# A selective-scan kernel: the product with B made in place, for two tiles in one GpSimd instruction

## The chip, the cores and the metric

The kernel runs on one core of a Trainium2 chip. Its engines each work through their own list of instructions in order and wait for one another by semaphores: TensorE (PE in the profile; its weight loads are PEld), VectorE (DVE), ScalarE (ACT), GpSimd (POOL) and SyncE (SP), whose queue here issues nearly all DMA transfers. The metric is the device time of one execution in microseconds. Three runs of the kernel before took 11,110.65, 11,111.8 and 11,118.07 us; the median is 11,111.8 us.

## What is computed

The input `x` is a batch of 8 images of 64 x 64 pixels with 96 channels, all float32. The reference applies two residual layers.

```python
# layer 0: x = x + SS2D(group_norm(x))
xz = einsum('bhwc,ec->bhwe', x, in_proj_w); xc, z = split(xz)      # 192 channels each
xa = silu(depthwise_conv3x3(xc) + conv_b)
xs = four orders of the 4096 pixels: rows, columns, and both reversed    # K = 4
x_dbl = einsum('bkdl,kcd->bkcl', xs, x_proj_w)                     # 6 dt rows, 16 B rows, 16 C rows
delta = softplus(dt_proj(dts) + dt_proj_b)
A = -exp(A_logs)                                                   # (K, 192, 16)
# at each of 4096 steps, for 192 channels x 16 states:
h = exp(delta * A) * h + (delta * u) * B
y = sum over the 16 states of h * C;   out = y + u * D
# the four orders are added, layer-normed, gated by silu(z), projected back to 96 channels

# layer 1: x = x + MLP(group_norm(x)), with up- and down-sampling by FFT filters around
h = coef0 + coef1 * (W1 x + b1) + coef2 * (W1 x + b1)**2;   W2 h + b2
```

Nearly all of the time goes to the scan `h = exp(delta * A) * h + (delta * u) * B`, which has 8 images x 4 orders x 192 channels x 16 states x 4096 steps.

## The kernel before

**Tiles.** One tile of the scan is 128 partitions by T = 1024 steps: 8 channels times 16 states. 192 channels make NT = 24 tiles for a chunk of 1024 steps; 4 chunks, 4 orders and 8 images make 3072 tiles in a row, in the list `tiles`. Each tile has a number `i` within its chunk, and the tiles of a chunk share a dictionary `got` with the chunk's inputs: `du` (delta times u, 192 x 1024, in DRAM), `dl` (delta), `br` and `cr` (the 16 rows of B and of C, repeated for the 8 channels, 128 x 1024 each).

**The steps of a tile.**
- `fetch` (line 1059): SP issues a DMA that reads 8 rows of `du` from DRAM and writes each of them 16 times, into the SBUF tile `dub`, 128 x 1024 (512 KB).
- `product_b` (1067): POOL multiplies `dub` by `br` into `bb`.
- `decay` (1071): PE spreads delta over the states by four matmuls into a PSUM tile `pd`, and ACT takes the exponential with the scale `neg_a`, in place.
- `scan` (1084): DVE runs the recurrence with `pd` as the factor and `bb` as the term. The result stays in `pd`, or goes to the SBUF tile `h` where the tile is marked `by_pool`: every third one (`i % 3 == 2`).
- `product_c` (1093): the result times `cr` gives `hc`. POOL does this for `by_pool` tiles, DVE for the others, 2048 of 3072.
- `hold` (1104): the last column is copied to `carry`, by ACT for `by_pool` tiles and else by DVE.
- `sums` (1119): PE adds the 16 states of two tiles at a time into the PSUM tile `py`; after eight tiles `store` copies it out.

**The order of the work** is written out by hand: the whole program is under a manual schedule, and the loop over `i` in its last part emits the steps of several tiles in each pass. In pass i, in this order: the loads of `before` where `i % 8 == 4`; the fetch of tile i + 6 (`FETCH`); `product_c` of tile i - 1 if it is POOL's; `product_b` of tile i + 3 (`LEAD`); `decay` of tile i + 1; `scan`, DVE's `product_c` and `hold` of tile i; then side work; and, in odd passes, `sums` of tiles i - 3 and i - 2. Two tiles of `pd` exist, four of `dub`, four of `bb`, four of `hc`, two of `h`.

**Side work.** The class `Side` holds generators for everything else: the loads, norms and convolutions of the next image (`front`), the layer norm and projection of the image before (`tail`), its MLP (`mlp`), and the preparation of the next chunk (`prepare`: `u`, `br`, `cr`, delta and `du`). A pass emits as many of their steps as a budget of estimated engine times (`CAPS`) allows. Where a pass gives PE too little, `turn_over` adds a matmul that nobody uses. The transfers of this side work are in SP's queue between the fetches.

**Buffers and waits.** Semaphore waits are derived from the use of tiles: a tile from a ring of four can be written again when the readers of the one four places before are done. So `fetch` of tile t waits for `product_b` of tile t - 4, and `product_b` of tile t waits for the scan of tile t - 4. A transfer also waits for the landing of the one that used its semaphore before; eight semaphores go round.

The functions that the change touches:

Of the kernel before, what the change touches and what calls it, by code (L numbers as in the profile page):

```python
# [8 lines left out]
F32 = mybir.dt.float32  # L9
AF = mybir.ActivationFunctionType  # L10
ALU = mybir.AluOpType
# [8 lines left out]
NS = 16  # L20
R = 6
K = 4
T = 1024
# [113 lines left out]
def kernel(ctx: ExitStack, tc: tile.TileContext, a: dict, out: bass.AP):  # L137
    nc = tc.nc
# [92 lines left out]
    sp = ctx.enter_context(tc.tile_pool(name="scan", bufs=3))  # L231
# [39 lines left out]
    def constants_in():  # L271
        nc.gpsimd.memset(xp, 0.0)
        raw["sel"] = tile_([128, 8, 128], "sel_0")
        for hf in range(2):
            nc.sync.dma_start(
                raw["sel"][64 * hf : 64 * hf + 64].rearrange("p j m -> p (j m)"),
                a["sel_b"][0:64, 0:2].rearrange("r q j m -> r (q j m)"),
            )
        raw["dt_b"] = tile_([C, K, HF], "dt_b")
        nc.sync.dma_start(raw["dt_b"], a["dt_b"])  # L280
        names = ("xp_dt", "xp_c", "xp_b")
        raw["xp"] = [tile_([128, K, Q3, R if n == "xp_dt" else NS], n) for n in names]
        ds = raw["ds"] = tile_([128, Q3, K], "ds")
        for hf in range(2):
            for q, r0, r1, f, c0 in pieces:
                rows, src = slice(64 * hf + r0, 64 * hf + r1), slice(c0, c0 + r1 - r0)
                for t, name in zip(raw["xp"], names):
                    nc.sync.dma_start(t[rows, :, q, :], a[name][src, :, f, 0 : t.shape[-1]])
                nc.sync.dma_start(ds[rows, q, :], a["ds"][src, f, :])
        for name, shape in (("coef", [128, 3, 3]), ("w2", [128, 3, C]), ("b2", [128, C])):  # L290
            raw[name] = tile_(shape, name)
            nc.sync.dma_start(raw[name], a[name])
# [748 lines left out]
    tiles = []  # L1041
    for b in range(images):
        for k in (1, 0, 2, 3):
            order = range(NCH) if k < 2 else range(NCH - 1, -1, -1)
            for n, c in enumerate(order):
                got = {}
                for i in range(NT):
                    q, n8 = divmod(i, 8)
                    s, j = n8 % 2, n8 // 2
# [6 lines left out]

    summed = set()

    def fetch(t):
        assert t["got"]["ready"]  # L1060
        t["dub"] = sp.tile([128, T], F32, tag="dub", name="dub", bufs=4)
        g = t["g"]
        nc.sync.dma_start(
            t["dub"], t["got"]["du"][None, 8 * g : 8 * g + 8, :].to_broadcast([NS, 8, T])
        )

    def product_b(t):
        t["bb"] = sp.tile([128, T], F32, tag="bb", name="bb", bufs=4)
        nc.gpsimd.tensor_tensor(t["bb"], t["dub"], t["got"]["br"], ALU.mult)  # L1069

    def decay(t):
        pd = t["pd"] = psd.tile([128, T], F32, tag="pd", name="pd")
        for hf in range(2):
            rows = slice(64 * hf, 64 * hf + 64)
            nc.tensor.matmul(  # L1075
                pd[:, MB * hf : MB * hf + MB],
                sel_b[rows, 4 * t["s"] + t["j"]].rearrange("p n c -> p (n c)"),
                t["got"]["dl"][rows, t["q"], :],
                start=True,
                stop=True,  # L1080
            )
        nc.scalar.activation(pd, pd, AF.Exp, scale=neg_a[:, t["k"], t["g"] : t["g"] + 1])  # L1082
# [10 lines left out]
    def product_c(t):  # L1093
        t["hc"] = sp.tile([128, T], F32, tag="hc", name="hc", bufs=4)
        (nc.gpsimd if t["by_pool"] else nc.vector).tensor_tensor(t["hc"], t["h"], t["got"]["cr"], ALU.mult)  # L1095
# [45 lines left out]
    def before(t):  # L1141

        if t["k"] == 0:
            return
        yp = t["got"]["yp"] = sp.tile([128, MB], F32, tag="yp", name="yp", bufs=2)
        if t["k"] == 1:
            q = t["q"]
            src = [
                u_dram[t["b"]][1][64 * q : 64 * q + 64, t["i0"] + MB * hf : t["i0"] + MB * hf + MB]
                for hf in range(2)  # L1150
            ]
        else:
            src = parts(t)
        for hf in range(2):
            nc.sync.dma_start(yp[64 * hf : 64 * hf + 64], src[hf])
# [14 lines left out]
    LEAD, FETCH = 3, 6  # L1170

    with tc.manual_schedule():
        side.queue = [bp.open("setup")]
        side.drain()
        constants_in()
        start, rest = front(0)
        side.queue = start[:-4]
        side.drain()
        side.queue = start[-4:] + [(8, 0, constants_of_scans), (8, 0, constants_of_mlp)]
        side.drain()  # L1180
        side.urgent = prepare(0, tiles[0]["k"], tiles[0]["i0"], tiles[0]["got"])
        side.queue, rest = rest[:4], rest[4:]
        while side.urgent or side.hurried:
            side.advance({e: (2 * most, 2 * most) for e, (_, most) in Side.CAPS.items()}, 2, 0)
        n = len(tiles)
        for i in range(FETCH):
            fetch(tiles[i])
            if i >= FETCH - LEAD:
                product_b(tiles[i - FETCH + LEAD])
        decay(tiles[0])  # L1190
        begin, *side.later = prepare(0, tiles[NT]["k"], tiles[NT]["i0"], tiles[NT]["got"])
        total = 1
        for i in range(n + 4):
            t = tiles[i] if i < n else None
            at = i % (NT * NCH * K)
            if t and t["i"] == 0:
                b = t["b"]
                if at == 0:
                    y_dram[b] = [dr.tile([DI, L], F32, tag=f"y{o}", name=f"y{o}") for o in range(2)]
                    side.begun, hasty = 0, sum(item[1] for item in rest) if b == 0 else 0  # L1200
                    side.queue += rest
                    down, end = [], []
                    if b:
                        keep = {}
                        side.queue += tail(b - 1, keep)
                        up, down, end = mlp(b - 1, keep)
                        side.queue += up
                    if b + 1 < images:
                        start, rest = front(b + 1)
                        side.queue += start[:2] + [i for two in zip(down, start[2:10]) for i in two] if b else start[:10]  # L1210
                        side.queue += start[10:] + rest
                        rest = []
                    else:
                        side.queue += down
                    side.queue += end
                    total = sum(item[1] for item in side.queue)
                if b == images - 1 and at == NT * NCH * (K - 1):
                    keep = {}
                    side.queue += tail(b, keep, pairs=False)
                    total = 0  # L1220

            ahead = 4 if i < 2 * NT else 8
            if (i + ahead) % NT == 0 and i + ahead + NT < n:
                nxt = tiles[i + ahead + NT]
                begin, *side.later = prepare(nxt["b"], nxt["k"], nxt["i0"], nxt["got"])
                side.urgent.append(begin)

            if i == 2:
                side.urgent.append(begin)
            if i == 4 or i and i % NT == 0:  # L1230
                side.urgent += side.later
                side.later = []
            if t and t["i"] % 8 == 4:
                before(t)
            if i + FETCH < n:
                fetch(tiles[i + FETCH])
            if 0 < i <= n and tiles[i - 1]["by_pool"]:
                product_c(tiles[i - 1])
            if i + LEAD < n:
                product_b(tiles[i + LEAD])  # L1240
            if i + 1 < n:
                decay(tiles[i + 1])
            if t:
                scan(t)
                if not t["by_pool"]:
                    product_c(t)
                hold(t)
            ends = i % 2 == 1 and 3 <= i <= n + 2
            adds = ends and tiles[i - 2]["j"] == 3 and tiles[i - 2]["k"]
            side.advance(  # L1250
                Side.CAPS,
                2 if not total or side.begun < max(hasty, total * at / 290) else 0,
                0 if 7 <= i % NT <= 21 else 1,
                0.95 * (bool(ends) + bool(adds)),
            )
            turn_over()
            if ends:
                sums(tiles[i - 3 : i - 1])
                if tiles[i - 2]["j"] == 3:
                    side.stores.append([g := store(tiles[i - 2]), next(g)])  # L1260
        up, down, end = mlp(images - 1, keep)
        side.queue += up + down + end
        side.drain()
# [89 lines left out]
```

## Time and profile before

| what | value |
|---|---|
| median of three runs | 11,111.8 us |
| profiled execution, from its first instruction to its last | 11,105.8 us |
| DVE busy | 10,207.5 us (92%) |
| POOL busy | 10,179.6 us (92%) |
| PE busy | 9967.9 us (90%) |
| ACT busy | 5910.6 us (53%) |
| DMA queue of SP | 86.5% of 16 engines' span, 2391.45 MB |
| `bb` products on POOL | 3072 of 2359 ns, 7173.5 us |
| `hc` products on POOL | 1024 of 2357 ns, 2413.9 us |
| scans on DVE | 3072 of 2280 to 2350 ns in four groups, 7163.7 us |
| `hc` products on DVE | 2048 of 1225 ns, 2508.4 us |

The profile is of one execution. It gives the time from its first to its last instruction; this is the profiled execution's own time in what follows, and the runs' median is 6 us above it. Busy time of an engine is the union of its instructions; waiting and issuing are not in it. In a line of a group of instructions, the part before the bar names line, engine, operation, output and inputs with their shapes and count; after it stand the busy time, the mean duration in ns, and the idle time of the engine just before these instructions with what ended it. In a line of waits, "DVE pd L1089 <- ACT carry L1108: 203.2, 414, 3.6" says that DVE's instruction at line 1089 sat idle until ACT's at line 1108 was done, for 203.2 us in total, 414 times, 3.6 us at most. "SPq" and the like are the engine's queue, in which it waits and issues.

### The profile page before, as it was taken

What the parts mean: (1) busy time and instruction counts of PE and PEld (TensorE: products, weight loads), DVE (VectorE), ACT (ScalarE), POOL (GpSimd) and SP (SyncE); (2) the same over time, 40 slices, a digit from 0 to 9 for tenths busy, and PEclk for the clock granted to TensorE, in tenths of its full rate; (3) what the DMA queues carried; (4) which work ended last, traced back from release to release, by engine and by line L of the source; (5) the groups of instructions that cost most, each with busy time, mean ns of one, the idle gap of its engine ahead of it and who ended that gap; (6) DMA issues with size and microseconds to landing.
All of it is one profiled execution on the core that took longest, in us unless ns stands there. A gap on an engine that the chain in (4) does not pass through costs nothing. (4 is left out here: it accounts for less than half of the span.)

```text
span 11105.8 us, 137238 instructions
## 1 busy us (share of the span) xinstructions
PE 9967.9 (90%) x45020; PEld 3204.6 (29%) x45020; DVE 10207.5 (92%) x7702; ACT 5910.6 (53%) x8218; POOL 10179.6 (92%) x4674
## 2 busy tenths in 40 slices
PE   8898888989889998999889998899988989889988
PEld 2222222322233222332223322233222332223325
DVE  6999999999999999999999999999999999999990
ACT  5455445656455564555545555455554655545543
POOL 5999999999999999999999999999999999999990
PEclk9999999999999999999999999999999999999998
DMA  6888898898988989888988989889898898988981
GB/s 174 215 208 224 209 231 209 217 227 232 233 209 216 225 231 225 212 218 224 240 217 215 224 221 244 209 219 225 217 243 210 217 228 218 247 206 216 227 214 48
DMA packets 1044463, 2401.27 MB, mean 216 GB/s; under 512 B 293820, under 2 KB 314556, under 8 KB 1043752
## 3 DMA queue, kind: packets, MB, share of 16 engines
q1 hardware_dynamic: 1042776, 2391.45, 86.5%
q8 instruction: 361, 5.91, 0.2%
q14 instruction: 350, 2.87, 0.1%
q10 hardware_dynamic: 976, 1.04, 0.0%
HBM read 1929.05 MB, written 328.73 MB: 203 GB/s over the span
## 5 line engine op out<-in xcount | busy, mean ns | idle before, releaser
L1069 POOL TENSOR_TENSOR bb<-dub,br 128x1024 f32<-128x1024 f32 x3072 | 7173.5, 2359 | 208.4 <-DMA dub<-du 149.2
L1082 ACT ACTIVATE pd<-pd,neg_a 128x1024 f32<-128x1024 f32 x3072 | 3340.7, 1088 | 4533.0 <-PE pd L1075 4489.8
L1075 PE MATMUL pd<-dl,sel_b 64*128 64x512 f32 x12288 | 3512.7, 645 | 987.2 <-DVE carry L1108 649.2
L1089 DVE TENSOR_TENSOR_SCAN pd<-pd,carry,bb 128x1024 f32<-128x1024 f32 x1536 | 3610.3, 2350 | 262.2 <-ACT carry L1108 127.9
L1095 POOL TENSOR_TENSOR hc<-h,cr 128x1024 f32<-128x1024 f32 x1024 | 2413.9, 2357 | 352.6 <-DVE h L1089 300.7
L1095 DVE TENSOR_TENSOR hc<-pd,cr 128x1024 f32<-128x1024 f32 x2048 | 2508.4, 1225 | 164.1 <-PE py L1127 20.0
L1075 PEld LDWEIGHTS pd<-dl,sel_b 64*128 64x128 f32 x12288 | 966.7, 186 | 3266.3 <-issue 1511.2
L1089 DVE TENSOR_TENSOR_SCAN h<-pd,carry,bb 128x1024 f32<-128x1024 f32 x768 | 1797.3, 2340 | 5.8 <-ACT pd L1082 5.6
L1127 PE MATMUL py<-hc,sel_r 128*32 128x512 f32 x12288 | 1715.0, 617 | 30.4 <-POOL hc L1095 30.2
L1089 DVE TENSOR_TENSOR_SCAN pd<-pd,bb 128x1024 f32<-128x1024 f32 x512 | 1172.5, 2290 | 98.6 <-ACT carry L1108 75.3
L1101 PE MATMUL idle<-sel_b,ident 128*128 128x512 f32 x1652 | 932.0, 646 | 8.0 <-DVE ty L720 5.9
L562 PE MATMUL pc<-pad,convr 96*128 96x512 f32 (+1 forms) x2304 | 858.3, 616 | 5.7 <-DVE e L585 3.6
L1089 DVE TENSOR_TENSOR_SCAN h<-pd,bb 128x1024 f32<-128x1024 f32 x256 | 583.6, 2280 | 26.0 <-ACT pd L1082 25.2
L1127 PEld LDWEIGHTS py<-hc,sel_r 128*32 128x32 f32 x12288 | 250.3, 109 | 1109.0 <-issue 854.5
L1031 POOL TENSOR_TENSOR u<-dl,u 128x512 f32<-128x512 f32 x384 | 485.0, 1271 | 79.2 <-DVE dl L1028 79.2
L862 PEld LDWEIGHTS p<-w2q,mq 128*100 128x100 f32 x4800 | 452.9, 168 | 274.6 <-issue 214.2
L855 PE MATMUL ph<-xu,w 96*128 96x500 f32 x960 | 504.9, 629 | 11.5 <-ACT mq L856 6.7
L862 PE MATMUL p<-w2q,mq 128*100 128x96 f32 x4800 | 511.5, 258 | 2.3 <-ACT mq L856 2.3
L562 PEld LDWEIGHTS pc<-pad,convr 96*128 96x128 f32 (+1 forms) x2304 | 266.3, 163 | 563.9 <-issue 552.8
L987 PE MATMUL px<-u,xp 64*64 64x512 f32 x1536 | 422.4, 627 | 2.4 <-issue 2.4
L1101 PEld LDWEIGHTS idle<-sel_b,ident 128*128 128x128 f32 x1652 | 249.8, 189 | 596.5 <-issue 522.4
L1012 PE MATMUL pv<-xd,dt_w 64*64 64x512 f32 x1536 | 394.4, 609 | 1.0 <-ACT xd L997 1.0
(153 smaller groups left out, 6707.9 us busy)
## 6 DMA issues: line engine op xcount, KB each, us to landing
dub<-du SPq DMA_DIRECT2D x3072, 512.0 KB
u<-u SPq DMA_DIRECT2D x256, 384.0 KB
du<-u SPq DMA_DIRECT2D x768, 128.0 KB
y<-yq SPq DMA_DIRECT2D x768, 128.0 KB
br<-xd SPq DMA_DIRECT2D x256, 256.0 KB
cr<-xd SPq DMA_DIRECT2D x256, 256.0 KB
yp<-y SPq DMA_DIRECT2D x384, 128.0 KB
yp<-u SPq DMA_DIRECT2D x192, 128.0 KB
```

Source lines behind the costliest of these rows:

```text
L562: nc.tensor.matmul(t[rows].rearrange("p (i j) -> p i j", i=8), weights[:, cs], v["pad"][:, 8 * blk + kw : 8 * blk + kw + 8, kh : kh + H], ...
L855: nc.tensor.matmul(t[:, :px], w1[:, m, :], xu, start=True, stop=True)
L862: nc.tensor.matmul(t[:SIDE, C * i : C * i + C], sq[:, m, row], w2q[:, m, :], start=(m == 0), stop=(m == 2))
L987: nc.tensor.matmul(p[rows], xp[rows, k, q, :], v["u"][rows, q, :], start=(q == 0), stop=(q == 2), skip_group_check=True,)
L1031: nc.gpsimd.tensor_tensor(v["u"][:, q, :], got["dl"][:, q, :], v["u"][:, q, :], ALU.mult)
L1069: nc.gpsimd.tensor_tensor(t["bb"], t["dub"], t["got"]["br"], ALU.mult)
L1075: nc.tensor.matmul(pd[:, MB * hf : MB * hf + MB], sel_b[rows, 4 * t["s"] + t["j"]].rearrange("p n c -> p (n c)"), t["got"]["dl"][rows, t[" ...
L1082: nc.scalar.activation(pd, pd, AF.Exp, scale=neg_a[:, t["k"], t["g"] : t["g"] + 1])
L1089: nc.vector.tensor_tensor_scan(t["h"][:, ::step], pd[:, ::step], t["bb"][:, ::step], 0.0 if t["first"] else held, ALU.mult, ALU.add)
L1095: (nc.gpsimd if t["by_pool"] else nc.vector).tensor_tensor(t["hc"], t["h"], t["got"]["cr"], ALU.mult)
L1101: nc.tensor.matmul(p, ident, sel_b[:, 0:4].rearrange("p j n c -> p (j n c)"), start=True, stop=True)
L1127: nc.tensor.matmul(py[r0 : r0 + 32], sel_r[:, t["j"], :], t["hc"][:, MB * hf : MB * hf + MB], start=(t["j"] == 0), stop=(t["j"] == 3 and t ...
```

## The change

`fetch` takes a pair of neighbouring tiles. It takes one SBUF tile of 128 x 2 x 1024 from a ring of four (`bb`; the ring `dub` is gone, and the memory is the same) and issues both tiles' transfers straight into its halves. `product_b` takes the pair and multiplies the whole tile by `br` in place, in one POOL instruction; `br` is read twice by a broadcast with step zero. The scans read their half of it. So a pair's buffer is held from its transfers to its second scan.

In the loop, the fetch of the pair (i + 6, i + 7) stands in every even pass i, and the product of the pair (i + 3, i + 4) in every odd pass. Before the loop, three pairs are fetched and two of them multiplied, where there were six fetches and three products. The transfers of the pair (p, p + 1) now wait for the scan of tile p - 7, the last reader of the buffer.

```diff
-    def fetch(t):
-        assert t["got"]["ready"]
-        t["dub"] = sp.tile([128, T], F32, tag="dub", name="dub", bufs=4)
-        g = t["g"]
-        nc.sync.dma_start(
-            t["dub"], t["got"]["du"][None, 8 * g : 8 * g + 8, :].to_broadcast([NS, 8, T])
-        )
-
-    def product_b(t):
-        t["bb"] = sp.tile([128, T], F32, tag="bb", name="bb", bufs=4)
-        nc.gpsimd.tensor_tensor(t["bb"], t["dub"], t["got"]["br"], ALU.mult)
+    def fetch(two):
+
+        assert two[0]["got"] is two[1]["got"] and two[0]["got"]["ready"]
+        both = two[0]["both"] = sp.tile([128, 2, T], F32, tag="bb", name="bb", bufs=4)
+        for j, t in enumerate(two):
+            t["bb"] = both[:, j, :]
+            g = t["g"]
+            nc.sync.dma_start(
+                t["bb"], t["got"]["du"][None, 8 * g : 8 * g + 8, :].to_broadcast([NS, 8, T])
+            )
+
+    def product_b(two):
+        both, br = two[0]["both"], two[0]["got"]["br"]
+        nc.gpsimd.tensor_tensor(both, both, br[:, None, :].to_broadcast([128, 2, T]), ALU.mult)
...
-        for i in range(FETCH):
-            fetch(tiles[i])
-            if i >= FETCH - LEAD:
-                product_b(tiles[i - FETCH + LEAD])
+        for i in range(0, FETCH, 2):
+            fetch(tiles[i : i + 2])
+            if i <= LEAD:
+                product_b(tiles[i : i + 2])
...
-            if i + FETCH < n:
-                fetch(tiles[i + FETCH])
+            if i % 2 == 0 and i + FETCH < n:
+                fetch(tiles[i + FETCH : i + FETCH + 2])
             if 0 < i <= n and tiles[i - 1]["by_pool"]:
                 product_c(tiles[i - 1])
-            if i + LEAD < n:
-                product_b(tiles[i + LEAD])
+            if i % 2 and i + LEAD < n:
+                product_b(tiles[i + LEAD : i + LEAD + 2])
```

## The prediction

> **What bounds the kernel now.** I read the page's busy shares first, then the busy time in the long middle stretch, then the groups of instructions, then the waits of each engine, since four resources turn out nearly equally full.
>
> ```profile
> span 11105.8 us, 137238 instructions
> ...
> PE 9967.9 (90%) x45020; PEld 3204.6 (29%) x45020; DVE 10207.5 (92%) x7702; ACT 5910.6 (53%) x8218; POOL 10179.6 (92%) x4674
> ```
>
> The stretch from 300 to 10,800 us, in which all scans but the first few run (columns: length; busy us of PE, PEld, DVE, ACT, POOL; clock; DMA share; GB/s):
>
> ```profile
> 300.00:10800.00 10500.00, 9450.66 (x42672) 2973.73 (x42670) 9957.59 (x7430) 5630.11 (x7788) 9960.40 (x4554) 0.99 0.89 222
> ```
>
> DVE and POOL are idle for 542 and 540 us of 10,500: two engines equally loaded, each handing tiles to the other. The groups show what they do, and the two other POOL rows are the yardsticks for the new instruction:
>
> ```profile
> L1069 POOL TENSOR_TENSOR bb<-dub,br 128x1024 f32<-128x1024 f32 x3072 | 7173.5, 2359 | 208.4 <-DMA dub<-du 149.2 <-DVE pd L1089 46.9 <-DVE h L1089 3.5
> L1095 POOL TENSOR_TENSOR hc<-h,cr 128x1024 f32<-128x1024 f32 x1024 | 2413.9, 2357 | 352.6 <-DVE h L1089 300.7 <-PE px L987 37.9 <-PE pd L1075 4.1
> L1031 POOL TENSOR_TENSOR u<-dl,u 128x512 f32<-128x512 f32 x384 | 485.0, 1271 | 79.2 <-DVE dl L1028 79.2
> L684 POOL TENSOR_TENSOR ty<-ty,ye 96x512 f32<-96x512 f32 x128 | 192.6, 1527 | 7.1 <-DMA ty<-y 7.1
> ```
>
> POOL waits mostly for DVE's scans (301 + 47 + 4 us) and for the broadcast transfer (149 us). Now who makes DVE wait:
>
> ```profile
> DVE pd L1089 <- ACT carry L1108: 203.2, 414, 3.6
> DVE pd L1089 <- ACT pd L1082: 113.8, 238, 8.0
> DVE pd L1089 <- POOL bb L1069: 40.2, 38, 2.3
> ...
> DVE h L1089 <- ACT pd L1082: 30.8, 17, 5.9
> ...
> DVE hc L1095 <- PE py L1127: 20.0, 8, 4.2
> ...
> DVE h L1089 <- POOL bb L1069: 0.8, 2, 0.5
> ```
>
> DVE waits for POOL's product only 41 us in 40 waits. It waits most for ACT. Much of that is built in: the scan that follows a `by_pool` scan starts a median 0.244 us late (gaps of every third scan, from the trace), because its decay on PE and ACT takes as long as one scan; over some 1000 scans, 244 us. Another 143 us are gaps under 150 ns. Of 542 us that leaves 155 us that could go at all. POOL's hidden way to DVE is PE: PE works in order, and its sums wait for POOL's `hc`, with the next decay behind them:
>
> ```profile
> PEld py L1127 <- POOL bb L1069: 125.1, 158, 1.5
> ...
> PEld py L1127 <- POOL hc L1095: 76.4, 63, 4.8
> ```
>
> In the 8 us before a late scan (gap over 150 ns, ended by ACT) I looked in the trace for the last PE wait over 0.3 us that POOL or a DMA ended. POOL's stand before 81 us of the scans' waits, DMAs' before 31 us; 12 us of the DVE products' waits go back to a late load of x. Last, SP, which issues every transfer in order:
>
> ```profile
> SPq L1063 <- POOL bb L1069: 4445.6, 2155, 7.0
> SPq L1063 <- DMA dub<-du: 253.3, 217, 2.9
> ```
>
> SP stands 4,446 us waiting for a product to free one of four `dub` buffers, and everything issued behind it waits too.
>
> The sum is made against the profiled span, 11,105.8 us; the median of the runs shown is 11,111.8, 6 us more, which I take as what lies around the span and keep.
>
> **The change part by part.**
>
> *One instruction for two.* From 512 to 1024 elements the product goes from 1271 to 2359 ns: 2.125 ns an element and 183 ns fixed. Two tiles: 2048 x 2.125 + 183 = 4535 ns against 4718, 183 ns less, 1536 times: 281 us off POOL. Neighbouring POOL instructions overlap by a median 42 ns, so where they stand back to back the gain is 141 ns, 217 us in all. In place is no unknown: L1031 writes over its own input. The repeated operand with its outer step of zero is not shown; the nearest row is L684, with a second dimension of 8 and a strided read, 1527 ns against 1271 for the plain row. If all that excess were due to the outer dimension it would be 32 ns a row, 64 ns a pair. Bounds: 4535 to, at L684's whole rate ((1527 - 183) / 512 = 2.625 ns an element), 5559 ns. I take 4535, since the inner runs stay contiguous like L1031's. This time is off the path except where DVE or PE waits for POOL.
>
> *DVE's direct waits for the product*, 41 us: bounds -41 and 0; I take -30, as POOL is 2 to 3% lighter and the product no longer waits for a scan to free a `bb` buffer (47 + 4 us of POOL's idle).
>
> *Scans late behind PE's waits for POOL*, 81 us: bounds -81 and 0; half, -40, since `hc` also waits for its own scan.
>
> *The transfers.* Before, the broadcast of tile t waits for the product of t-4. Now both transfers of a pair (p, p+1) wait for the scan of p-7, on DVE. Measured from the end of that scan, SP now issues p's at a median 2.5 us and p+1's at 5.3 us; in the new order both could go at about 0.1 and 0.7 us (an issue takes 0.53 us). No transfer is added. p+1's issue moves one iteration up, past that iteration's stores of `du`, `y` and `z` and loads of `yp`, `u` and x, which then stand behind up to 512 KB more: 2.1 us at 222 / 0.89 = 249 GB/s; but SP itself reaches them sooner. Bounds: all of the 31 + 12 = 43 us gone, or doubled. I take -10.
>
> *The later start of the first tile of a pair.* It must wait for the second tile's transfer and for the whole 4.5 us. A landing takes a median 5.3 us and in 95% under 9.4; the order allows 21.6 us (median) from that scan's end to the scan of p, against 0.7 + 9.4 + 2.1 + 4.5 = 16.7: covered. If the products began no sooner than now, their first tile would come 2.18 us later; today's distance from product to scan is under that in 49 of 1485 pairs, 72 us short in sum. Bounds 0 and +72; I take +10, because products may now start earlier.
>
> *POOL's queue.* The product of p+1 moves ahead of POOL's `hc` of tile p-3 where that is POOL's (512 times), and ahead of POOL's side work (L1031, L684) of that iteration. That `hc` can start only when its scan ends, about 13.7 us (four tiles of 3.42) after the scan that frees the pair; by then the pair is done at 0.7 + 5.3 + 2.1 + 4.5 = 12.6 us. Behind a landing of 9.4 us it is 3 us late, and PE's sums, then the decay, then DVE wait. That case lies within the +72 and the half that I left of the 81.
>
> *A third semaphore on the scan of every pair's first tile* (transfer, product, ACT): 1536 sequencer steps of 21 ns, +32 at most. They run while the preceding product (1.23 us) or scan (2.34 us) executes; without that cover they would cost the 32. I take 0.
>
> Order and number of PE, DVE and ACT instructions do not change, the prologue issues the same six transfers and one more product early, and the tail after 10,836 us has no product.
>
> Sum: -30 - 40 - 10 + 10 = -70; 11,111.8 - 70 = 11,042. Best ends: -41 - 81 - 43 = -165, of which the 155 us above allow -155. Worst ends: +72 + 32 + 43 = +147, 11,259.
>
> *A rule against the change.* POOL's product takes 2328 to 2457 ns over all 3072, and DVE's scans 2231 to 2360: neither shows a stretch of standing blocked by the other. "SBUF — State Buffer", section "SBUF: two separate sides", has VectorE and GpSimd share one port pair under an exclusive lock for the whole instruction, against DVE operations with two SBUF inputs; by it a 4.5 us product would block such an operation twice as long. In the loop each large DVE row reads one operand from PSUM (pd, pc, pz, pv, pn), so by the rule too the sum stays 11,042.
>
> **The rivals.**
> 1. The forecast: POOL gets spare time, DVE stays the bound and loses part of its waits. 11,042, own range 10,990 to 11,089. 0.44.
> 2. POOL was a full partner in the bound. For it: 540 us idle against 542. Then all of DVE's avoidable 155 us go: 10,957. Against: only 41 us of direct waits. 0.22.
> 3. The saved time lies off the path altogether and becomes POOL waiting for scans: 11,090 to 11,134. For it: POOL's largest wait is already for DVE's scan. 0.13.
> 4. Slower: the pair hands over too coarsely. Place: the first scan of a pair and the `hc` behind the product, when a landing is late. Price +72 for the first tiles, and if `hc` coming 2.2 us later doubles what reaches the scans through PE in one case in three, +27: 11,211. It decides from some 1.4 us of added delay per short pair on, where 49 x 1.4 equals the 70 gained. For it: DMA is 89% busy. Against: the allowance of 21.6 us. 0.16.
> 5. The paired instruction is dear, at L684's rate: 841 ns over two single ones, +1292 us of POOL; at most 540 us of idle absorb it: 11,864 to 12,404. It decides from 4.72 us a pair on. 0.05.
>
> **How the numbers follow.** 0.2% of the time, 22 us, is about what a measurement of this kernel can tell from no change. Faster: cases 1 and 2, 0.66; same: case 3, 0.13; slower: cases 4 and 5, 0.21. The range reaches from the end of case 2 to nearly the end of case 4, 10,960 to 11,200; case 5 and the outer edges of 2 and 4 are left out, under 0.2 together.
>
> **What the profile after would show.** L1072 (the new product) x1536 at about 4.53 us; POOL busy near 9,900 to 9,960 us and its wait for DVE's `h` up from 301 us to 450 or more; DVE busy unchanged at about 10,207; DVE's waits for the product under 20 us; PE's waits at the sums for POOL down from 201 us; SP's wait at the broadcast no longer for POOL but for DVE. Wrong if the pair takes over 4.72 us, if POOL's waits for the broadcast rise well over 149 us, or if DVE's waits for the product rise.

## The result, and the profile after

The kernel with the pair takes 11,225.76 us (median of four runs, 11,223.16 to 11,236.84) against 11,114.93 us before (four runs, 11,110.65 to 11,122.17). The ratio is 1.0100, with a 95% interval of 1.0087 to 1.0113: 1% slower, where 0.6% faster was forecast. The profiled spans stand at 11,105.8 and 11,223.9 us, 118 us apart, and it is these two that are compared below. One execution of `single_fetch7`, a kernel further down, took 27,461 us at a granted clock of 0.34, where its other four took 11,065 to 11,095 at 0.98; its ratio leaves that one out, and the cause is not known.

The page of the kernel after, its busy shares:

```profile
span 11223.9 us, 133053 instructions
...
PE 10040.6 (89%) x45020; PEld 3217.4 (29%) x45020; DVE 10208.7 (91%) x7702; ACT 5904.8 (53%) x8218; POOL 9958.0 (89%) x3138
```

DVE has done the same work (10,207.5 us before), POOL 222 us less, and the program is longer. No engine has become the bound by its sum: waiting has grown. The same stretch as before, 300 to 10,800 us, with the same columns:

```profile
300.00:10800.00 10500.00, 9419.10 (x42216) 2952.74 (x42208) 9852.17 (x7356) 5574.15 (x7722) 9637.90 (x3014) 0.99 0.90 220
```

DVE is idle for 648 us of it (542 before), POOL for 862 (540). The groups of the new product and of POOL's `hc`:

```profile
L1072 POOL TENSOR_TENSOR bb<-bb,br 128x2048 f32<-128x2048 f32 x1536 | 6942.8, 4531 | 382.1 <-DMA bb<-du 370.4 <-issue 6.0 <-POOL u L1031 4.0
...
L1098 POOL TENSOR_TENSOR hc<-h,cr 128x1024 f32<-128x1024 f32 x1024 | 2412.6, 2356 | 529.9 <-DVE h L1092 360.0 <-PE px L987 81.5 <-PE idle L1104 26.5
```

The instruction costs what was forecast, 4531 ns. In front of it POOL now stands 370 us waiting for the broadcast, 149 before. The waits of DVE and PE for POOL, from the view of all waits:

```profile
DVE pd L1092 <- ACT pd L1085: 288.2, 386, 8.0
...
PEld py L1130 <- POOL hc L1098: 173.6, 109, 4.7
...
DVE pd L1092 <- POOL bb L1072: 92.4, 69, 3.8
...
PE py L1130 <- POOL hc L1098: 84.4, 61, 3.8
...
DVE pd L1092 <- issue: 81.1, 238, 2.0
```

And, from the same view of before, the row for PE's `sums` that stands beside the 76.4 us of the weight loads:

```profile
PE py L1127 <- POOL hc L1095: 30.2, 25, 3.9
```

The two lines of PE are its `sums` waiting for POOL's `hc`: 258 us together, against 76.4 + 30.2 = 107 before. DVE's direct waits for the product rose from 41 to 96 us (3.5 of them ahead of scans into `h`). The 203 us that DVE waited for ACT's `carry` have no row of that name after; "issue" and "ACT pd" have grown instead. That most of this is another name for the same waits is argued, not shown: the scans behind `by_pool` tiles, where those waits stood, start a median 0.15 us (i % 6 = 0) and 0.18 us (i % 6 = 3) late now, 0.16 and 0.25 before.

**Where DVE waits.** The order of the kernel repeats every six tiles: pairs every two, POOL's `hc` every three. So I added up DVE's idle time in the trace by the place in the six, over tiles 100 to 3060. It grew from 536 to 649 us, by 113 of the 118, and in three places only: ahead of the scans with i % 6 = 3 ("scans 3" below) from 184 to 257, ahead of the scans with i % 6 = 0 ("scans 0") from 121 to 162, and ahead of DVE's `hc` of tiles with i % 6 = 3 from 17 to 53. The other places fell by 37 together.

**What POOL does in that time.** POOL's timeline before (start, length, instruction, number of them back to back; in brackets the idle time ahead and what ended it):

```profile
7299.66 2.34 POOL L1095 TENSOR_TENSOR hc<-h,cr 128x1024 f32<-128x1024 f32 x1
7301.97 6.98 POOL L1069 TENSOR_TENSOR bb<-dub,br 128x1024 f32<-128x1024 f32 x3
7309.22 2.35 POOL L1095 TENSOR_TENSOR hc<-h,cr 128x1024 f32<-128x1024 f32 x1 [0.27 <-DVE h L1089]
```

And after:

```profile
7306.11 2.35 POOL L1098 TENSOR_TENSOR hc<-h,cr 128x1024 f32<-128x1024 f32 x1 [3.96 <-DVE h L1092]
7308.42 8.99 POOL L1072 TENSOR_TENSOR bb<-bb,br 128x2048 f32<-128x2048 f32 x2
7317.36 2.36 POOL L1098 TENSOR_TENSOR hc<-h,cr 128x1024 f32<-128x1024 f32 x1
7319.66 4.54 POOL L1072 TENSOR_TENSOR bb<-bb,br 128x2048 f32<-128x2048 f32 x1
```

Before, three products lie between two `hc`. After, it is two pairs, then one: four products in one half of the six tiles and two in the other. Write `hc(5)` for the `hc` of tile 5. `hc(2)` and two pairs take 2.36 + 2 x 4.53 - 0.08 of overlap = 11.3 us, and DVE delivers the next tile for POOL's `hc` after three scans, a median 10.04 us (before). So POOL is late for `hc(5)` by its own queue, with no transfer late at all. Measured from one `hc` to the next, the half with the two pairs went from a median 9.84 to 11.30 us, and the other from 10.36 to 8.45. In the short half POOL waits (its idle time ahead of that `hc` went from 165 to 500 us); ahead of the other it has almost none left (188 to 30). The `hc` of an odd tile now ends a median 4.29 us after its scan, 2.64 before.

Why that reaches DVE: `sums` takes tiles 4 and 5 together, in pass 7, two passes after the scan of tile 5. PE works in order and waits there for `hc(5)`; the next decay in PE's list is that of tile 9, and 9 % 6 = 3 is where DVE waits. An even tile's `hc` is summed three passes after its scan and has one more pass of time.

### The profile page after: what moved, and what is told of

It is laid out like the page before. It is cut to its first block, busy times and chain, and to the rows that moved or that the text cites. A ratio compares the mean times of both kernels' runs of the same rounds, so it can differ in the third digit from the quotient of the medians.

```text
span 11223.9 us, 133053 instructions
## 1 busy us (share of the span) xinstructions
PE 10040.6 (89%) x45020; PEld 3217.4 (29%) x45020; DVE 10208.7 (91%) x7702; ACT 5904.8 (53%) x8218; POOL 9958.0 (89%) x3138
## 5 line engine op out<-in xcount | busy, mean ns | idle before, releaser
L1072 POOL TENSOR_TENSOR bb<-bb,br 128x2048 f32<-128x2048 f32 x1536 | 6942.8, 4531 | 382.1 <-DMA bb<-du 370.4
L1130 PE MATMUL py<-hc,sel_r 128*32 128x512 f32 x12288 | 1774.0, 615 | 84.9 <-POOL hc L1098 84.4
```

Of the source, the lines that this page charges most:

```text
L1072: nc.gpsimd.tensor_tensor(both, both, br[:, None, :].to_broadcast([128, 2, T]), ALU.mult)
L1130: nc.tensor.matmul(py[r0 : r0 + 32], sel_r[:, t["j"], :], t["hc"][:, MB * hf : MB * hf + MB], start=(t["j"] == 0), stop=(t["j"] == 3 and t ...
```

## The experiments

Each ratio is to the kernel before, measured beside it. "Order" in the table is the number of products between POOL's `hc` calls, first half and second half of the six tiles. Idle times are DVE's, us, over tiles 100 to 3060, worked out from the traces; the last two columns come from the views of waits.

| kernel | ratio [95%] | order | DVE idle | ahead of scans 3 | scans 0 | its `hc` of 3 | PE waits at `sums` for POOL's `hc` | POOL waits for the broadcast |
|---|---|---|---|---|---|---|---|---|
| before | 1 | 3 + 3 | 536 | 184 | 121 | 17 | 107 | 149 |
| the change | 1.0100 [1.0087, 1.0113] | 4 + 2 | 649 | 257 | 162 | 53 | 258 | 370 |
| single_in_place | 0.9977 [0.9968, 0.9987] | 3 + 3 | 516 | 177 | 132 | 17 | 134 | 126 |
| products_apart | 0.9976 [0.9967, 0.9986] | 3 + 3 | 520 | 193 | 123 | 17 | 117 | 124 |
| two_products | 1.0057 [1.0042, 1.0072] | 4 + 2 | 599 | 274 | 96 | 52 | 287 | 162 |
| reversed | 1.0140 [1.0125, 1.0155] | 4 + 2 | 683 | 292 | 167 | 53 | 280 | 332 |
| late_first_transfer | 1.0146 [1.0131, 1.0161] | 4 + 2 | 706 | 380 | 102 | 52 | 441 | 345 |
| paired_0 | 1.0016 [1.0007, 1.0025] | 3 + 3 | 573 | 196 | 180 | 17 | 30 | 152 |
| paired_2 | 1.0076 [1.0061, 1.0091] | 4 + 2 | 613 | 283 | 98 | 54 | 355 | 235 |
| paired_4 | 1.0021 [1.0010, 1.0033] | 3 + 3 | 550 | 207 | 113 | 17 | 142 | 227 |
| hc_first | 1.0071 [1.0055, 1.0088] | 2 + 4 | 615 | 151 | 208 | 17 | 3 | 155 |
| even_pool | 1.0126 [1.0111, 1.0141] | 2 + 4 | 679 | 235 | 73 | 17 | 71 | 317 |
| single_fetch7 | 0.9965 [0.9951, 0.9979] | 3 + 3 | 495 | 170 | 115 | 17 | 91 | 37 |
| lump_fetch7 | 1.0028 [1.0016, 1.0039] | 4 + 2 | 568 | 239 | 92 | 52 | 231 | 58 |

**The parts one by one.** The change has four parts: the product in place (a ring that transfers fill and the scans free), the transfers in pairs, the coarse order of POOL's queue, and the one instruction that waits for two landings. Three theories stood ahead of the runs: A, the order and the late first tile of a pair; B, transfers that come too late; C, the long instruction itself and its third semaphore. The first two parts can be made alone. In `single_in_place`, the kernel before is changed only in its ring: eight single tiles, multiplied in place.

```diff
-        t["dub"] = sp.tile([128, T], F32, tag="dub", name="dub", bufs=4)
+        t["bb"] = sp.tile([128, T], F32, tag="bb", name="bb", bufs=8)
...
-        t["bb"] = sp.tile([128, T], F32, tag="bb", name="bb", bufs=4)
-        nc.gpsimd.tensor_tensor(t["bb"], t["dub"], t["got"]["br"], ALU.mult)
+        nc.gpsimd.tensor_tensor(t["bb"], t["bb"], t["got"]["br"], ALU.mult)
```

> The kernel before, with one edit: the product is written over the broadcast of du, tile by tile, in a ring of eight single buffers; its transfer waits for the scan of tile t-8. No pairs, and each product at its old place on GpSimd. Three theories for the 1.0% that the changed kernel lost. A: on GpSimd the product of the second tile now stands ahead of hc of every odd tile (tiles 5, 11, .. of 6), and the first tile of a pair waits for the whole 4.5 us; then this run, which has none of that, is 0.990 to 1.001 of before. B: the transfers come too late, since they now wait for VectorE's scans and stand in SP's queue behind stores that are not ready; then 1.003 to 1.010, and GpSimd's wait for the transfer is well over the 149 us of before. C: the long instruction itself and the third semaphore on the scans; then 0.997 to 1.002.

`products_apart` keeps the changed kernel's pair ring and paired transfers, and makes single products in the old places:

```diff
-        both, br = two[0]["both"], two[0]["got"]["br"]
-        nc.gpsimd.tensor_tensor(both, both, br[:, None, :].to_broadcast([128, 2, T]), ALU.mult)
+        br = two[0]["got"]["br"]
+        for t in two:
+            nc.gpsimd.tensor_tensor(t["bb"], t["bb"], br, ALU.mult)
...
-            if i % 2 and i + LEAD < n:
-                product_b(tiles[i + LEAD : i + LEAD + 2])
+            if i + LEAD < n and i:
+                product_b(tiles[i + LEAD : i + LEAD + 1])
```

> The changed kernel with its pairs of transfers and its ring of four pairs, but the product made tile by tile, in two instructions, each at its old place on GpSimd (tile i+3 in pass i). A: 0.990 to 1.002 of before, and the gap ahead of scans 3, 9, .. (i mod 6 = 3) falls back from 257 us to about 184 us. B: 1.005 to 1.012, as in the changed kernel, with some 370 us of GpSimd waiting for the transfers. C: 0.997 to 1.002.

`two_products` goes one step further towards the change: the two products stand together at the pair's place, as two instructions.

```diff
-        both, br = two[0]["both"], two[0]["got"]["br"]
-        nc.gpsimd.tensor_tensor(both, both, br[:, None, :].to_broadcast([128, 2, T]), ALU.mult)
+        br = two[0]["got"]["br"]
+        for t in two:
+            nc.gpsimd.tensor_tensor(t["bb"], t["bb"], br, ALU.mult)
```

> The changed kernel, but the product of a pair made by two instructions one after the other at the place of the one: the order on GpSimd is that of the changed kernel, no instruction is longer than 2.4 us, the scans have two semaphores as before, and GpSimd is as busy as before (about 10,180 us). A: 1.006 to 1.02 of before: the order is what costs, and without the shorter time of the paired instruction no less. B: 1.007 to 1.015. C: 0.997 to 1.003.

The two that leave POOL's order alone are faster than before, by 0.23 and 0.24%. Waits in `products_apart`:

```profile
POOL bb L1073 <- DMA bb<-du: 123.6, 78, 6.0
...
PEld py L1131 <- POOL hc L1099: 79.2, 59, 4.0
...
PE py L1131 <- POOL hc L1099: 37.3, 28, 3.1
```

And in `two_products`:

```profile
PEld py L1131 <- POOL hc L1099: 178.9, 92, 6.2
...
POOL bb L1073 <- DMA bb<-du: 161.5, 110, 7.3
...
PE py L1131 <- POOL hc L1099: 107.7, 53, 5.3
```

Nothing but the place of every other product differs between them, and it costs 0.8% (1.0057 is just under the 1.006 at which A's range began, and outside C's range): PE's waits for POOL's `hc` go from 117 to 287 us, the idle time ahead of scans 3 from 193 to 274, and `hc(5)` ends a median 4.29 us after its scan, 2.46 in `products_apart`. POOL's wait for the broadcast hardly rises (124 to 162), so this part of the loss is the order's. It is about two thirds of the 1.24% between `products_apart` and the change.

**An order without the lump.** If pairs every two and `hc` every three do not fit, `by_pool` on even tiles alone should. `even_pool`:

```diff
-                    tiles[-1]["by_pool"] = i % 3 == 2
+                    tiles[-1]["by_pool"] = i % 6 in (2, 4)
```

> The changed kernel with another third of the tiles on GpSimd for the product by C: tiles 2 and 4 of every six in place of 2 and 5, so that no odd tile's hc is GpSimd's. Same counts on every engine. A: the gap ahead of the scans that follow them falls, and the time is 0.990 to 1.003 of before. B: 1.005 to 1.012, with GpSimd's wait for transfers at 300 us or more. C: 1.006 to 1.012. Against A one thing is unknown: two scans at a distance of two and four tiles, where it was three, may bunch GpSimd's work.

Its time is a miss for the theory of the order, though PE's waits at `sums` did fall, to 71 us. DVE now waits elsewhere:

```profile
DVE pd L1092 <- ACT pd L1085: 478.2, 778, 8.0
```

This is the wait of the scans with i % 6 = 3 and 5, behind `by_pool` tiles, for their decays: 235 and 220 us. The edit also moves DVE's own work: two of every three scans from tile 2 to tile 4 now have no `hc` of DVE's behind them, where it was every third throughout. So it does not say what the order is worth. POOL's wait for the broadcast, 317 us, is also nearly that of the change, so what the two landings cost may be in it as well. What exactly makes those decays late stayed open.

**What the one instruction adds.** The change is 0.43% slower than `two_products`, though its instruction is shorter. Either its first tile comes too late for its scan, or its wait for both landings holds POOL's queue. `reversed` makes two products in the pair's place, the second tile's first: like the pair it must see the second landing before it can finish the first tile, but with two full instructions.

```diff
-        for t in two:
+        for t in two[::-1]:
             nc.gpsimd.tensor_tensor(t["bb"], t["bb"], br, ALU.mult)
```

(on `two_products`.)

> As in two_products, two instructions at the place of the one, but the second tile of the pair first. So the first tile is ready only after both, as in the changed kernel, and both transfers must have landed, while no instruction is long and the scans keep two semaphores. two_products stood at 1.006 of before and the changed kernel at 1.010. If the first tile's lateness makes that difference: 1.010 to 1.014, and VectorE's wait for the product ahead of scans 0, 6, .. goes from 4 us to 80 us or more. If it is the form of the one instruction (its length, its third semaphore): 1.004 to 1.008.

```profile
POOL bb L1073 <- DMA bb<-du: 332.3, 178, 8.3
...
DVE pd L1093 <- POOL bb L1073: 86.6, 63, 3.9
```

It comes near both waits of the change (332 against 370 us, 87 against 96) and is 0.83% slower than `two_products`. Against it the change gains 0.4%: that is what one shorter instruction in place of two is worth here, its third semaphore included, so theory C is not what loses. To part the two reasons, `late_first_transfer` makes the products in their natural order and issues the second tile's transfer first. Then the first product, at the head of POOL's queue, waits for the later landing, but it is still the first tile that is ready first.

```diff
-        for j, t in enumerate(two):
+        for j, t in reversed(list(enumerate(two))):
```

(on `two_products`.)

> two_products with one edit: SP issues the transfer of a pair's second tile ahead of that of the first. GpSimd still makes the first tile's product first, so that one now waits for both transfers, but it does not stand behind the other product. two_products stood at 1.006 of before, reversed (both transfers and both products ahead of the first tile) at 1.014. If waiting for the second transfer is what makes a first tile late: 1.011 to 1.015, with GpSimd's wait for transfers at 300 us or more. If standing behind the other tile's 2.36 us is: 1.005 to 1.008.

```profile
POOL bb L1073 <- DMA bb<-du: 344.9, 180, 8.4
...
PEld py L1131 <- POOL hc L1099: 272.1, 128, 7.1
...
PE py L1131 <- POOL hc L1099: 168.8, 84, 6.2
```

It costs as much as `reversed`, with DVE's direct waits for the product at only 15.5 us. So waiting for the later landing is dear even where the first tile is not late: it holds POOL's queue, `hc` stands behind it, and PE behind that. In `reversed`, and in the change, part of the same delay shows as DVE's direct wait instead.

**Which pair does it.** Of the three pairs in six tiles only (6k + 2, 6k + 3), in the example tiles 8 and 9, changes the order to 4 + 2, because its second product passes the `hc` of an odd tile. `paired_0`, `paired_2` and `paired_4` make one of the three as a pair in one instruction and leave the others single (`product_b` takes one tile or two):

```diff
...
-            if i % 2 and i + LEAD < n:
-                product_b(tiles[i + LEAD : i + LEAD + 2])
+            if i and i + LEAD < n:
+                two = (i + LEAD) % 6 - (i + LEAD) % 2 == 0
+                if i % 2 or not two:
+                    product_b(tiles[i + LEAD : i + LEAD + 1 + two])
```

(with 2 and 4 in place of 0 in the others.)

> As products_apart (0.998 of before), but tiles 0 and 1 of every six get one paired instruction at the changed kernel's place; the other four keep single products at their old places. On GpSimd these two follow directly on hc of the last by_pool tile before. If the lateness of the first tile costs there: 1.002 to 1.006, with VectorE waiting 70 us or more for the product ahead of scans 0, 6, .. If the order of hc alone matters: 0.995 to 0.999.

> As products_apart, but tiles 2 and 3 of every six get one paired instruction at the changed kernel's place. There the product of tile 3 of the next six goes ahead of hc of tile 5, which TensorE's sums wait for, with the decay of tile 3 behind them. If that order is the cause of 80 us, as two_products against products_apart says: 1.003 to 1.008, with TensorE's waits for GpSimd's hc at the sums up from about 117 us to 230 us or more, and the gap ahead of scans 3, 9, .. from 193 to about 260 us. If it is the lateness of first tiles alone: 0.996 to 1.000.

> As products_apart, but tiles 4 and 5 of every six get one paired instruction at the changed kernel's place, where no hc of GpSimd's stands behind it within its six tiles' order and no hc directly ahead. Both parts of the explanation say that it costs nothing here, and GpSimd is some 70 to 95 us less busy: 0.995 to 0.9985. If pairing costs wherever it is done: 1.001 to 1.004.

From the 0.9976 of `products_apart`, `paired_0` costs 0.40%, `paired_2` 1.00% and `paired_4` 0.45%. `paired_2` alone brings the three marks of the order: 355 us of PE's waits, 283 us ahead of scans 3, and the `hc` of tile 3 at 54 us.

```profile
PEld py L1133 <- POOL hc L1101: 216.9, 96, 6.0
...
PE py L1133 <- POOL hc L1101: 137.9, 69, 5.1
```

`paired_0` (1.0016, just under the 1.002 at which its range for a late first tile began) loses at the scans 0, which wait 101 us for the pair itself. `paired_4` was a miss: it was expected to gain like `products_apart`, and lost. Its pair waits for the broadcast 173 us, where all products of `products_apart` together wait 124, and its scans 4 wait 27 us for the pair.

```profile
POOL bb L1073 <- DMA bb<-du: 173.2, 82, 8.4
```

In its trace all 173 us end with the landing of the second tile's transfer, some 120 of them after the first tile's had landed. That this wait is what the kernel loses by is argued from `late_first_transfer`, not shown for this kernel.

**The order turned round.** In `hc_first` the pair (8, 9) is emitted one pass later, behind `hc(5)`:

```diff
-            if i % 2 and i + LEAD < n:
+            if i % 2 and i + LEAD < n and (i + LEAD) % 6 != 2:
                 product_b(tiles[i + LEAD : i + LEAD + 2])
+            if i and i % 6 == 0 and i + 2 < n:
+                product_b(tiles[i + 2 : i + 4])
```

> The changed kernel with one edit: the paired product of tiles 2 and 3 of every six is emitted one pass later, behind GpSimd's hc of tile 5 instead of ahead of it. If hc standing behind that product delays TensorE's sums and the next decay: TensorE's waits for GpSimd's hc at the sums fall from 258 us to 150 us or less and the gap ahead of scans 3, 9, .. from 257 to 200 us or less. In exchange that pair is ready only some 6.9 us (2.36 + 4.53) after scan 5 ends, where VectorE wants it after 7.5 us, so VectorE's wait for the product ahead of scans 2, 8, .. goes up from 4 us. Time 1.002 to 1.010; over 1.012 if the second effect wins.

```profile
DVE pd L1092 <- POOL bb L1072: 154.1, 113, 3.9
...
DVE h L1092 <- POOL bb L1072: 49.9, 57, 3.6
...
PEld py L1130 <- POOL hc L1098: 3.3, 4, 1.6
```

PE's waits for `hc` are gone, 258 to 3 us, the scans 3 wait 151 us, less than before the change, and DVE's `hc` of tile 3 is back at 17. So those marks do hang on what stands ahead of `hc(5)`. The delay has moved: two pairs now stand between `hc(5)` and `hc(8)`, and the pair (12, 13) behind them. DVE waits 204 us directly for products, 139 of them ahead of the scans 0, 50 ahead of the scans 2, whose pair is made a pass late, and 15 ahead of the scans 4. It is 0.3% better than the change and still slower than before.

**A faster version, and the order by itself.** `single_fetch7` is `single_in_place` with the transfers one pass earlier, which a ring of eight allows.

```diff
-    LEAD, FETCH = 3, 6
+    LEAD, FETCH = 3, 7
```

> single_in_place (0.998 of before) with each transfer issued one pass earlier (FETCH 7 in place of 6), which the ring of eight allows: it waits for the scan of the pass before. If late transfers still cost something: 0.994 to 0.997 and GpSimd's wait for transfers falls from 126 us to 60 us or less. If not: 0.997 to 0.999; if the earlier place in SP's queue holds up what stands behind it: 0.999 to 1.002.

```profile
POOL bb L1068 <- DMA bb<-du: 37.1, 40, 5.9
```

At 0.9965 it has the lowest ratio of this study (span 11,063.3 us), below the kernel before and the change. The interval overlaps that of `single_in_place`, so that seven is better than six is not shown by the times, only that POOL waits less. In it the transfers are hardly a cause of anything, and so it is a clean place for the order: `lump_fetch7` makes the same single products, two in each odd pass.

```diff
-            if i + LEAD < n:
-                product_b(tiles[i + LEAD])
+            for j in (LEAD,) if i == 0 else (LEAD, LEAD + 1) if i % 2 else ():
+                if i + j < n:
+                    product_b(tiles[i + j])
```

> single_fetch7 (0.9965 of before, GpSimd waits 37 us for transfers) with the products in the changed kernel's order, as single instructions: four products, then two, between GpSimd's hc of every third tile, where it was three and three. The transfers still go tile by tile, one pass earlier than in the pairs. If the order costs by itself, since hc of tile 2 and four products (5 x 2.36 = 11.8 us) outlast the three scans (some 10.2 us) before hc of tile 5: 1.001 to 1.005, with the gap ahead of scans 3, 9, .. up from 170 us to 220 us or more. If it costs only where a late transfer holds up the product in front of hc: 0.996 to 0.999.

```profile
PEld py L1126 <- POOL hc L1094: 139.7, 55, 6.2
...
PE py L1126 <- POOL hc L1094: 91.6, 41, 5.3
...
POOL bb L1068 <- DMA bb<-du: 57.7, 59, 5.8
```

With the transfers on time, the order alone costs 0.63% (0.9965 to 1.0028), through `hc` and PE's `sums` as before (91 to 231 us), and the three marks are there (scans 3 from 170 to 239 us, the `hc` of tile 3 from 17 to 52).

**The account.** In place and fetched in pairs: -0.24% (`products_apart`). Products two by two, so 4 + 2: +0.81% (`two_products`). Waiting for both landings and the first tile later: +0.83% (`reversed`). One shorter instruction in place of two: -0.40% (the change). By the intervals each step is known to about 0.2%. They add up to the measured +1.00% by construction, since they lie in a row. In the second step DVE's idle time grew by 81 us ahead of the scans 3 and by 36 ahead of its `hc` of tile 3, and fell by 38 elsewhere; the 36 are a second semaphore (last section), not a late `hc`, and no run separates what the two cost.

## Why the prediction was wrong, step by step

- **The instruction, and POOL's relief.** Forecast 4535 ns and 217 to 281 us; measured 4531 ns and 222 us. Right, and rival 5 is out with it. 4531 is under the sum from the plain rows, so neither the in-place form nor the operand with step zero is seen to cost. The Trainium skill ("GPSIMD Engine Reference", section "3.1 Elementwise — side-by-side cycle accounting") gives 4497 ns for a `tensor_tensor` add of 2048 float32 elements; this case's product took 4531, within 1% of it. The time that POOL gained went into more waiting on both sides: its wait for `h` rose to 360 us (450 or more were forecast), and its wait for the broadcast by 221.
- **POOL's queue.** This is the step that failed. It held the finish of one pair, 12.6 us after the scan that frees its buffer, against the scan that `hc` needs, at 13.7, and found `hc` not delayed. That sum has one landing and one product in it. What stands ahead of `hc(5)` in POOL's own queue, counted from the start of `hc(2)`, is `hc(2)` and two pairs, 11.3 us, in place of `hc(2)` and three products, 9.3 us in the timeline above; three scans take 10.04. So a spare 0.7 us became a lack of 1.3. The two rows that it needed, 2357 and 4535 ns, were in the prediction, and the six tiles in the order of the loop. Measured, the pair's product ends a median 17.5 us after that scan, not 12.6. The Trainium skill ("PSUM — Partial Sum Buffer", section "Engine vs sequencer instructions") calls GpSimd's queue strict FIFO; the timeline above agrees: the second `hc` starts at 7317.36 us, as the two pairs ahead of it end.
- **DVE's direct waits** (-30) **and the first tile's later start** (+10). Measured +55 (41 to 96 us), nearly all ahead of the scans 0. The bound of +72 for the first tile held it. The distance from the product to the scan of the first tile fell from a median 6.0 to 4.1 us; the product was to start earlier, and starts at the same median 13.0 us after the scan that frees the buffer (its end, 15.4 before and 17.5 now, less its duration).
- **Scans late behind PE's waits for POOL** (-40). The wrong sign: PE's waits for `hc` rose from 107 to 258 us, and the idle time ahead of the scans 3 by 73. Spare time on POOL came in the half of the six tiles where it was not needed.
- **The transfers** (-10). They are issued earlier, as was said: SP starts on p a median 0.08 us after the scan that frees the buffer (2.50 before) and on p + 1 0.84 us after it (5.34). In a quarter of the pairs p's start is over 2.5 us late; SP now stands longer at stores whose data is not ready. And p + 1 landed a mean 7.1 us after it had been issued, 5.9 before. The wait for the second tile's landing was named and held to be covered (16.7 us against 21.6); that POOL's queue stands still behind it got no price of its own. POOL's wait for the broadcast went from 149 to 370 us. In the trace all 370 end with the landing of the second tile's transfer, some 270 of them after the first tile's had landed. The text of the prediction named a rise of this wait as what would prove it wrong. SP's queue after:

```profile
SPq L1066 <- DVE pd L1092: 1857.3, 545, 10.0
...
SPq L1034 <- POOL u L1031: 737.1, 235, 8.9
SPq L1166 <- ACT yq L1163: 675.8, 246, 17.9
```

  Its wait at the fetch is for DVE, as forecast. At the two stores, the last two lines, it waited 157.5 and 120.1 us before.
- **A third semaphore on the scan** (0). No cost is seen: ahead of scans 2 and 4, which have it too, the idle time fell (24 to 13 and 19 to 14 us). But a wait that the prediction did not look for has a cost: DVE's `hc` of tile 3, which follows its scan at once, waits for a second semaphore wherever the order is 4 + 2, and 36 of the 113 us are there.
- **The rivals.** Rival 4, that the pair hands over too coarsely at its first scan and at the `hc` behind it, was right in place. That its 11,211 is near the measured 11,225.76 is in part luck: it counted 72 us for first tiles and 27 through PE, where the idle time grew by 41 us ahead of the scans 0 and by 73 ahead of the scans 3, with 36 ahead of DVE's `hc` of tile 3, which it did not name. Its condition was wrong: it was made to need a late landing, and most of the loss comes without one. It had a chance of 0.16, and its price lay above the end of the range, 11,200.
- **Two readings of the rows before.** The 201 us of PE's waits for POOL at the sums included the row `PEld py <- POOL bb`, 125.1 us, though `sums` does not read `bb`; it is 29.7 after, and the waits for `hc` alone are compared here. The 244 ns taken as built in for each scan behind a `by_pool` scan is a median over two places that differ, 246 ns at the scans 3 and 164 at the scans 0; by these, some 210 us are built in, and the most that could go was nearer 190 us than 155. Neither changes the forecast's sign.

## What to carry to other kernels

Where two kinds of work with different periods share an in-order queue, write down the queue for one common period (six tiles here) and add up what stands ahead of each instruction that someone waits for; a gain in the engine's sum says nothing of it. An instruction that takes the data of two transfers starts after the later landing (all 370 us of POOL's waits here), and all that is queued behind it starts late too; price that by the waits of the whole queue, not by those of its own reader. The part of a change that needs no new order may be worth keeping alone: the ring in place gave 0.9977 here, and 0.9965 filled a pass earlier, where the whole change gave 1.0100.

## What the runs showed of the hardware

- **A second semaphore on DVE.** The `hc` of tile 3 starts a median 34 ns after its scan where it waits for the scan alone, and 104 ns where POOL's semaphore is added: 70 ns, 493 times in the stretch counted, 35 us. The six kernels with the order 4 + 2 show it, and none of the others. DVE's `hc` of tile 4, which always waits for a second semaphore, starts a median 104 ns after its scan in the thirteen kernels that have it. Why the order brings the wait is argued, not shown: `hc(9)` overwrites the buffer of `hc(5)`, and only where tile 9's product stands behind `hc(5)` in POOL's queue has tile 9's scan already waited for both.
- **POOL's long instruction.** All 1536 pairs took 4495 to 4619 ns, and DVE's scans 2231 to 2359 beside them (2231 to 2360 before). Long or short, no stretch shows POOL or DVE held up by the other: DVE's busy time is 10,208.7 us with pairs and 10,209.8 with two products at the same place.
- **One resource, two faces.** POOL's lateness shows as a wait of PE for `hc` or as a direct wait of DVE for the product: 258 and 96 us in the change, 3 and 204 in `hc_first`, which differs from it in the order of POOL's queue alone.
